# A graph-layer kernel: VectorE's queue alone in the planner's order, GpSimd's transfers ordered by the framework

## The chip, the cores and the metric

The kernel runs on one core of a Trainium2 chip. The time is device microseconds from the first to the last instruction, the median of three runs. Times inside the kernel come from one profiled execution of it.

## What is computed

There are 16 graphs of 1024 nodes with 64 channels. Layer 0 is a dense step and layer 1 a ragged one: for each node and each channel it takes three quantiles over the node's neighbours. Cut to what matters:

```
h = max(layernorm(x), 0);  x = x + (adj / max(rowsum(adj), 1)) @ h            # layer 0
h = max(layernorm(x), 0)
nb      = (adj > 0) without the diagonal                                       # layer 1
removed = every skip-th neighbour, in nodes with more than 10 (and its transpose)
agg     = 0.25 * q25 + 0.5 * q50 + 0.25 * q75   # sorted values of the neighbours left and the node itself
x = x + mask * (relu((h + agg) @ W1 + b1) @ W2 + b2)
```

Most nodes have few neighbours and a few have many: the edge probability falls with the square root of the node's number.

## The kernel before, in words

**Layer 0.** A batch is one graph. Eight row tiles of its adjacency (`at`, 128x1024, five buffers) are loaded by SyncE. ScalarE takes their signs (`sg`), VectorE turns these into lists of neighbours (`rec`, 32 MAX8 instructions a batch), TensorE transposes the tiles (`pt`), ScalarE copies them out (`att`), and TensorE multiplies by the normed features (`ps_small`). VectorE adds the residual and norms once more (`ln_v`). The rows go to two tables in DRAM: `tab` by plain transfers, and `srt`, in which the nodes of four batches are sorted by their number of neighbours, by scatters on GpSimd (`srt<-row,to`, eight a batch, 128 in all).

**Layer 1.** Four batches make a group, and there are four groups. A group reads its sorted records (`recs`), makes the indices of neighbours on VectorE (`keys`, `idx`), and is then cut into ten jobs by list length (`CAPS`). A job has T columns of 128 nodes with n-1 neighbours each. Its neighbours' rows are fetched by T(n-1) gathers on GpSimd (`places<-tab,idx`): 15, 10, 8, 14, 6, 20, 16, 18, 12 and 5 gathers in the ten jobs, with T = 1, 1, 1, 2, 1, 4, 4, 6, 6 and 5. VectorE sorts the rows with a sorting network (`rem`, then min and max between `places` and `other`) and weights them (`w`, `prod`). Then the job's `layers` follow: TensorE sums (`pt`), ScalarE copies (`ot`), TensorE (`ps_small`), ScalarE (`hid`), TensorE, ScalarE (`y`). VectorE adds the residual to `y`, and GpSimd scatters it to the output (`out_dram<-y,nodes_i`, T stores a job). The nodes with the longest lists, of all groups, are four more jobs of 88, 31, 24 and 20 gathers (`lplaces`). They use the room that layer 0 leaves, so that they start after it.

**Who sets the order.** All parts are generators, and a small planner (`Plan`) chooses at each step which of them goes on. It holds a clock for each engine, and for each tile a time at which it is expected to be ready (`at(tile)`), from costs written out by hand; `room(name, bufs)` is the time at which a buffer comes free. A generator yields the engine it needs and a time from which it wants to go on. The planner takes the one with the earliest start, then the lowest rank. Slack is given by constants that are added to `at`. Three of them stand in the change: `LOOSE` (TensorE's start of `layers`, and VectorE's addition to `y`), `ROWS` (the row scatters, the gather of a group's or a long list's adjacency rows, and the `drop` scatters) and `LATE` (the stores of `y`):

```
LOOSE = 15.0
ROWS = 7.0
LATE = 25.0
```

The order in which the planner writes the instructions is what the framework sees. On engines that are named in `manual_schedule` the queue keeps that order. On the others the framework sorts the queue by a schedule of its own. Before, VectorE (DVE) and GpSimd (Pool) are named, and TensorE, ScalarE and SyncE are the framework's.

Each engine works through its queue in order, so an instruction that waits holds all that stand behind it. Between two scatters to the same table that follow each other, the kernel writes a small memset to `turn` on GpSimd. `places` has three buffers, `S` (the job's own rows) four, `y` six.

Nearly all instructions pass through the wrapper `Timed`, so they share one line, L227, in the profile. They are told apart by their tiles.

Of the kernel before, what the change touches and what calls it, by code (L numbers as in the profile page):

```python
# [9 lines left out]
F32 = mybir.dt.float32  # L10
# [8 lines left out]
P = 128  # L19
# [190 lines left out]
INF = float("inf")  # L210
BREATH = 0.8
AHEAD = 8
SLACK = 2.0
LOOSE = 15.0
ROWS = 7.0
LATE = 25.0


class Timed:
# [13 lines left out]
class Plan:  # L233
# [24 lines left out]
    def room(self, name, bufs):  # L258

        tiles = self.slots.get(name, ())  # L260
        if len(tiles) < bufs:
            return 0.0
        old = tiles[-bufs]
        return INF if self.users[old] else max(self.used.get(old, 0.0), self.ready.get(old, 0.0))

    def at(self, *tiles):
        return max(self.ready.get(t.tensor.name, INF) for t in tiles)
# [60 lines left out]
@with_exitstack  # L328
def kernel(
    ctx: ExitStack,  # L330
    tc: tile.TileContext,
    x: bass.AP,
    adj: bass.AP,
    nodemask: bass.AP,
    w1: bass.AP,
    b1: bass.AP,
    w2: bass.AP,
    b2: bass.AP,
    out: bass.AP,
):  # L340

    nc = tc.nc
    B = x.shape[0]

    flags = ctx.enter_context(tc.tile_pool(name="flags", bufs=1))
    go = flags.tile([P, 1], I32, name="go")

    with tc.manual_schedule(engines={mybir.EngineType.DVE, mybir.EngineType.Pool}):
        list_path(tc, x, adj, nodemask, w1, b1, w2, b2, out, go)
    taken = nc.values_load(go[0:1, 0:1], min_val=0, max_val=1)
    with tc.If(taken > 0):  # L360
        with tc.For_i(0, B, 1) as b:
            dense_path(tc, b, x, adj, nodemask, w1, b1, w2, b2, out)
# [3 lines left out]
def list_path(ctx, tc, x, adj, nodemask, w1, b1, w2, b2, out, go):  # L366
# [3 lines left out]
    CO = w2.shape[1]  # L370
# [19 lines left out]
    mlp = ctx.enter_context(tc.tile_pool(name="mlp", bufs=2))  # L390
# [88 lines left out]
    new, free, room, at = plan.tile, plan.release, plan.room, plan.at  # L479
# [56 lines left out]
    def known(st, *names):  # L536

        return max(at(st[name]) if name in st else INF for name in names)
# [176 lines left out]
    def endings(pool, now):  # L715

        for b, st in enumerate(batch):
            now[0] = b
            g, gb = divmod(b, GB)
            yield "ACT", lambda: known(st, "rec", "row") if st["listed"] == NT else INF  # L720
            rec, total, row = st["rec"], st["total"], st["row"]

            for t in range(NT):
                nc.scalar.activation(
                    row[:, t, R0:R0 + 8 * NSEG], rec[:, t, :], AF.Relu, bias=before[:, t:t + 1]
                )


            yield "DVE", always
            found = new(pool, [P, NT, 8 * NSEG], BF, "found", 1)  # L730
            nc.vector.tensor_scalar(found, rec, 0.0, None, op0=OP.is_gt)
            d = new(tiny, [P, NT], F32, "d", 2)
            nc.vector.tensor_reduce(d, found, AX.X, OP.add)
            full = new(tiny, [P, NT], F32, "full", 2)
            nc.vector.tensor_reduce(
                full, found.rearrange("p t (s e) -> p t s e", e=8)[:, :, :, 7], AX.X, OP.max
            )
            nc.vector.scalar_tensor_tensor(d, full, float(STEPS[0]), d, op0=OP.mult, op1=OP.max)
            nc.vector.tensor_scalar(d, d, float(STEPS[0]), None, op0=OP.min)
            for s in STEPS[1:]:  # L740
                nc.vector.scalar_tensor_tensor(d, total, float(s), d, op0=OP.is_gt, op1=OP.add)
            free(rec)
            free(total)
            hot = new(tiny, [P, CLS, NT], BF, "hot", 2)
            nc.vector.tensor_tensor(
                hot, cls, d.unsqueeze(1).to_broadcast([P, CLS, NT]), OP.is_equal
            )
            yield "PE", lambda: max(at(hot), room("ps_small", 3))
            pc = new(ps_s, [P, HALF], F32, "ps_small", 3, users=1)
            K = CLS * NT  # L750
            flat = hot.rearrange("p c t -> p (c t)")
            nc.tensor.matmul(pc[:, :K], earlier, flat, start=True, stop=True)
            nc.tensor.matmul(pc[:, K:2 * K], ones, flat, start=True, stop=True)
            yield "DVE", lambda: at(pc) + SLACK
            base = new(tiny, [P, K], F32, "base", 2)
            nc.vector.tensor_tensor_scan(
                base, pc[:, K:2 * K], zeros[:, :K], 0.0, op0=OP.add, op1=OP.add
            )
            nc.vector.tensor_tensor(base, base, pc[:, K:2 * K], OP.subtract)
            nc.vector.tensor_tensor(base, base, pc[:, :K], OP.add)  # L760
            free(pc)
            nc.vector.tensor_tensor(base, base, flat, OP.mult)
            pos = new(tiny, [P, NT], F32, "pos", 2)
            nc.vector.tensor_reduce(pos, base.rearrange("p (c t) -> p t c", t=NT), AX.X, OP.add)
            low = new(tiny, [P, NT], I32, "low", 2)
            nc.vector.tensor_copy(low, pos)
            nc.vector.tensor_scalar(low, low, LSUB - 1, None, op0=OP.bitwise_and)
            nc.vector.tensor_scalar(
                pos, pos, float(GB), float(LSUB * gb), op0=OP.mult, op1=OP.add
            )  # L770
            to = new(pool, [P, NT], I32, "to", 2)
            nc.vector.scalar_tensor_tensor(to, low, float(1 - GB), pos, op0=OP.mult, op1=OP.add)
            for t in range(NT):
                yield "POOL", lambda: max(at(to), at(row)) + ROWS if "normed" in st else INF
                scatter(srt[g], row[:, t, :], to[:, t:t + 1], sorts[g])
            free(row)
            progress["batches"] = b + 1
# [8 lines left out]
    def scatter(dst, src, idx, others):  # L786
        if plan.last is others:
            nc.gpsimd.memset(turn, 0.0)
        ins = nc.gpsimd.indirect_dma_start(
            out=dst, out_offset=bass.IndirectOffsetOnAxis(ap=idx, axis=0),  # L790
            in_=src, in_offset=None,
        )

        for other in others:
            tc.declare_no_dep(ins.ins, other, reason="rows of their own")
        others.append(ins.ins)
        plan.last = others

    class Job:
# [160 lines left out]
        def layers(self, terms, sources):  # L960

            T, R = self.T, terms[0][0].shape[1]
            yield "PE", lambda: max(at(*sources) + LOOSE, room("y", 6), room("pt", 2))
            y = new(mlp, [P, T, CO], F32, "y", 6, users=1)
            for t0 in range(0, T, 4):
                ts = range(t0, min(t0 + 4, T))
                M = len(ts) * P
# [2 lines left out]
                pt = new(ps_t, [P, HALF], F32, "pt", 2, users=1)  # L970
# [33 lines left out]
                free(py)  # L1004
            yield "DVE", lambda: at(y) + LOOSE
            nc.vector.tensor_tensor(y, y, self.S[:, :, X1:R0], OP.add)
            if self.short:
                free(self.S)
            for t in range(T):
                yield "POOL", lambda: at(y) + LATE  # L1010
                scatter(out_rows, y[:, t, :], self.nodes_i[:, t:t + 1], scatters)
            free(y)
            progress["jobs"][self.g] += 1
# [1 line left out]
    def group(g):  # L1015
# [17 lines left out]
        )  # L1033
        nodes_i = new(grp, [P, NTAU], I32, "nodes_i", 2)
        nc.vector.tensor_copy(nodes_i, nodes)
        yield "POOL", lambda: at(nodes_i) + ROWS
        full = new(grp, [P, N], F32, "gat_rows", 1)
        gather(full, adj_rows, nodes_i[:, 0:1])
        yield "DVE", always
# [22 lines left out]
        drop = new(tiny, [P, 2, 2], F32, "drop", 2)  # L1062
# [42 lines left out]
        for e in range(2):  # L1105
# [1 line left out]
                nb, cum, skip[:, e, :], None, op0=OP.is_lt, op1=OP.add,  # L1107
                accum_out=drop[:, 0, e:e + 1],
            )
        yield "POOL", lambda: at(drop) + ROWS  # L1110
        for e in range(2):
            nc.gpsimd.indirect_dma_start(
                out=pairs[:R * TS * PW, :],
# [9 lines left out]
        for i, ts in enumerate(classes):  # L1123
            n, T = CAPS[ts[0]] + 1, len(ts)
# [8 lines left out]
    def long_lists(pool):  # L1133
# [4 lines left out]
        for l, K in enumerate(LONG):  # L1138
# [12 lines left out]
            nc.vector.tensor_tensor(nodes, node, noff[:, 1:2], OP.add)  # L1151
            nodes_i = new(pool, [P, 1], I32, "lnodes_i", 4)
            nc.vector.tensor_copy(nodes_i, nodes)
            yield "POOL", lambda: max(at(nodes_i) + ROWS, room("lat", 1))
            full = new(pool, [P, N], F32, "lat", 1)
            gather(full, adj_rows, nodes_i)
            yield "DVE", lambda: at(full)
# [61 lines left out]
    for g in range(NG):  # L1219
        plan.add(group(g), -2000)  # L1220
    with tc.tile_pool(name="lay0", bufs=2) as pool:

        for stream, first in (
            (endings, 0), (channels, 1), (products, 2), (transposes, 4), (listing, 5),
            (beginnings, 6), (loads, 7), (signs, -15),
        ):
            now = [0]
            plan.add(stream(pool, now), lambda first=first, now=now: 10 * now[0] + first)
        plan.run(lambda: progress["batches"] == B)
    with tc.tile_pool(name="long", bufs=1) as pool:  # L1230
        plan.add(long_lists(pool), -1500)
        plan.run()
# [292 lines left out]
```

## Time and profile before

| | before |
|---|---|
| time, median of 3 runs | 1949.79 us (1947.86 to 1966.94) |
| span of the profiled execution | 1953.2 us |
| busy: TensorE, VectorE, ScalarE, GpSimd | 818.3, 1252.1, 607.3, 965.2 us |
| gathers `places`, 496 | 493.1 us, mean 994 ns |
| gathers `lplaces`, 163 | 172.3 us, mean 1057 ns |
| scatters `srt`, 128 | 125.4 us, mean 980 ns |
| stores of `y`, 124 of the groups | 129.6 us, mean 1045 ns |
| `turn` memsets, 200 | median 118 ns |

The busy shares say how much of the span an engine works, not what sets the end. Layer 0 with groups 0 and 1 fills the time to about 1080 us. From there on there are the long lists and groups 2 and 3. For a change of order one must look at each stage for the waits of the engine that carries it, and at what stands behind a waiting instruction in its queue.

### The profile page before, as it was taken

The page shows a single profiled execution, that of the slowest core. Times are in us where ns is not written, and L with a number is a line of the kernel's source. Part 1 is how long each engine was busy: PE and PEld are TensorE (multiplying, and loading weights), DVE is VectorE, ACT ScalarE, POOL GpSimd, SP SyncE. Part 2 cuts the span into 40 slices and gives each one's busy share as a digit, 9 for nine tenths or more (in the row PEclk, how much of TensorE's full clock was granted, in tenths as well). Part 3 has the DMA queues.
Part 4 walks back from the last instruction along what each step waited for, and adds up shares of the span by engine and source line. Part 5 has one row for each costly group of instructions (what it writes and reads, how often), then busy time and mean ns, then how long its engine had stood idle before and what let it go on. Part 6 is the DMA issues. An engine that isn't in the chain of part 4 may idle for free.

```text
span 1953.2 us, 15147 instructions
## 1 busy us (share of the span) xinstructions
PE 818.3 (42%) x3336; PEld 518.3 (27%) x3336; DVE 1252.1 (64%) x4090; ACT 607.3 (31%) x1874; POOL 965.2 (49%) x1140
## 2 busy tenths in 40 slices
PE   6778651345688236611577001000001458142155
PEld 3334421223355013410245000000001237132134
DVE  7766877636676557954642396747935779785290
ACT  7888744225465435513333000000000011010011
POOL 0123255534434654347525625478775546747723
PEclk8978875667788678755777555555555557555556
DMA  4545633213344323422201201111111101111100
GB/s 159 160 123 167 182 103 83 64 47 75 93 123 126 91 77 117 105 74 60 56 23 37 56 19 32 30 40 22 24 27 36 25 17 25 25 43 32 24 7 14
DMA packets 119013, 129.09 MB, mean 66 GB/s; under 512 B 68306, under 2 KB 86866, under 8 KB 118914
## 3 DMA queue, kind: packets, MB, share of 16 engines
q1 hardware_dynamic: 86178, 86.58, 15.6%
q0 software_dynamic: 32736, 41.47, 9.4%
q14 instruction: 71, 0.58, 0.1%
q8 instruction: 28, 0.46, 0.1%
HBM read 108.70 MB, written 19.28 MB: 66 GB/s over the span
## 4 chain that ended last, share of the span: by engine, by line
DVE 34%; PE 16%; issue 15%; another core or an unknown queue 14%; ACT 9%; POOL 8%; DMA 2%; SPq 0%; DVEq 0%; POOLq 0%; ACTq 0%
PE ps_small L227 9%; PE pt L227 7%; DVE other L227 5%; DVE places L227 5%; DVE rec L227 4%; POOL lplaces L227 3%; POOL places L227 2%; DVE lplaces L227 2%; DVE long_other L227 2%; ACT ln_sq L227 2%; ACT sg L227 2%; DVE sg L227 2%; POOL out_dram L227 2%; ACT att L227 2%
## 5 line engine op out<-in xcount | busy, mean ns | idle before, releaser
L227 POOL DMA_INDIRECT places<-tab,idx x496 | 493.1, 994 | 263.6 <-issue 141.7
L227 PE MATMUL pt<-ident,prod 128*128 128x128 f32 (+1 forms) x736 | 155.7, 371 | 553.1 <-DVE prod L227 350.2
L227 PE MATMUL ps_small<-att,h 128*65 128x512 f32 x512 | 269.8, 677 | 63.3 <-ACT h L227 42.8
L227 PEld LDWEIGHTS pt<-ident,prod 128*128 128x128 f32 (+1 forms) x736 | 127.2, 254 | 586.0 <-issue 210.5
L227 PE MATMUL pt<-ident,at 128*128 128x128 f32 x1024 | 184.9, 329 | 170.8 <-ACT att L227 83.5
L227 POOL DMA_INDIRECT srt<-row,to x128 | 125.4, 980 | 261.0 <-ACT row L227 158.6
L227 POOL DMA_INDIRECT out_dram<-y,nodes_i x124 | 129.6, 1045 | 210.9 <-issue 72.2
L227 POOL DMA_INDIRECT lplaces<-tab,lidx x163 | 172.3, 1057 | 73.0 <-issue 47.8
L227 PEld LDWEIGHTS pt<-ident,at 128*128 128x128 f32 x1024 | 139.6, 167 | 225.0 <-ACT att L227 106.8
L227 DVE MAX8 rec<-sg 128x8 f16<-128x256 f16 x512 | 180.2, 414 | 13.2 <-remote 5.8
L227 ACT COPY att<-pt 128x512 f32<-128x512 f32 x256 | 142.3, 583 | 130.9 <-remote 79.8
L227 ACT COPY ot<-pt 128x128 f32<-128x128 f32 (+3 forms) x56 | 22.4, 399 | 426.6 <-issue 175.3
L227 ACT ACTIVATE sg<-at 128x1024 f16<-128x1024 f32 x128 | 134.9, 1055 | 40.8 <-DVE rec L227 19.0
L227 DVE TENSOR_TENSOR sg<-sg,keyed 128x1024 f16<-128x1024 f16 x128 | 87.3, 682 | 81.0 <-ACT sg L227 80.8
L227 PEld LDWEIGHTS ps_small<-att,h 128*65 128x65 f32 x512 | 78.7, 159 | 208.8 <-issue 137.8
L227 PE MATMUL ps_small<-ot,w_sb 128*128 128x128 f32 (+3 forms) x112 | 56.9, 602 | 121.7 <-ACT ot L227 89.1
L227 DVE TENSOR_TENSOR other<-places,other 128x64 f32<-128x64 f32 (+6 forms) x204 | 69.8, 342 | 39.3 <-DVE places L227 11.6
L227 PE MATMUL ps_small<-w_sb,hid 128*128 128x64 f32 x256 | 68.6, 360 | 58.4 <-issue 43.0
L227 ACT ACTIVATE y<-ps_small,recs 128x64 f32<-128x64 f32 x124 | 31.5, 312 | 187.2 <-PE ps_small L227 66.3
L227 ACT ACTIVATE wu<-wu 128x39 f32<-128x39 f32 (+9 forms) x40 | 9.4, 235 | 249.7 <-issue 130.5
L227 DVE TENSOR_TENSOR places<-places,other 128x64 f32<-128x64 f32 (+2 forms) x208 | 62.4, 309 | 25.4 <-DVE other L227 10.2
L227 PEld LDWEIGHTS ps_small<-w_sb,hid 128*128 128x128 f32 x256 | 51.1, 246 | 87.7 <-issue 53.3
(208 smaller groups left out, 1652.2 us busy)
## 6 DMA issues: line engine op xcount, KB each, us to landing
at<-in_adj_dram SPq DMA_DIRECT2D x128, 512.0 KB
places<-tab,idx POOLq DMA_INDIRECT x496
tab<-row SPq DMA_DIRECT2D x16, 264.0 KB
xt<-in_x_dram SPq DMA_DIRECT2D x16, 256.0 KB
S<-srt SPq DMA_DIRECT2D x8, 390.0 KB
lplaces<-tab,lidx POOLq DMA_INDIRECT x163
recs<-srt SPq DMA_DIRECT2D x4, 544.0 KB
S<-srt SPq DMA_DIRECT2D x8, 260.0 KB
```

What stands on the lines that cost most here:

```text
L227: ins = getattr(self._engine, op)(*args, **kwargs)
```

## The change

GpSimd is taken out of `manual_schedule`: its transfers are now ordered by the framework, as TensorE's and ScalarE's are. VectorE's queue stays in the planner's order. The three constants become one of 7.0, which brings the addition to `y` and the stores closer behind the rows they need in the plan; the gathers of adjacency rows and the `drop` scatters have no slack any more. `y` has four buffers in place of six, in the kernel and in the planner's condition. The aim is to let the framework put transfers where their data are ready, and to end a job soon after its sort, so that its buffers come free.

```
-LOOSE = 15.0
-ROWS = 7.0
-LATE = 25.0
+LOOSE = 7.0
...
-    with tc.manual_schedule(engines={mybir.EngineType.DVE, mybir.EngineType.Pool}):
+    with tc.manual_schedule(engines={mybir.EngineType.DVE}):
...
             for t in range(NT):
-                yield "POOL", lambda: max(at(to), at(row)) + ROWS if "normed" in st else INF
+                yield "POOL", lambda: max(at(to), at(row)) + LOOSE if "normed" in st else INF
                 scatter(srt[g], row[:, t, :], to[:, t:t + 1], sorts[g])
...
-            yield "PE", lambda: max(at(*sources) + LOOSE, room("y", 6), room("pt", 2))
-            y = new(mlp, [P, T, CO], F32, "y", 6, users=1)
+            yield "PE", lambda: max(at(*sources) + LOOSE, room("y", 4), room("pt", 2))
+            y = new(mlp, [P, T, CO], F32, "y", 4, users=1)
...
             for t in range(T):
-                yield "POOL", lambda: at(y) + LATE
+                yield "POOL", lambda: at(y) + LOOSE
                 scatter(out_rows, y[:, t, :], self.nodes_i[:, t:t + 1], scatters)
...
-        yield "POOL", lambda: at(nodes_i) + ROWS
+        yield "POOL", lambda: at(nodes_i)
         full = new(grp, [P, N], F32, "gat_rows", 1)
...
-        yield "POOL", lambda: at(drop) + ROWS
+        yield "POOL", lambda: at(drop)
...
-            yield "POOL", lambda: max(at(nodes_i) + ROWS, room("lat", 1))
+            yield "POOL", lambda: max(at(nodes_i), room("lat", 1))
```

## The prediction

> **What bounds the kernel now.** I read the page first (busy shares and slices), then the busy times of five stretches of the span, then VectorE's waits in two windows, then single lines of the timeline.
>
> ```profile
> PE 818.3 (42%) x3336; PEld 518.3 (27%) x3336; DVE 1252.1 (64%) x4090; ACT 607.3 (31%) x1874; POOL 965.2 (49%) x1140
> ...
> DVE  7766877636676557954642396747935779785290
> ...
> POOL 0123255534434654347525625478775546747723
> PEclk8978875667788678755777555555555557555556
> ```
> No engine is full. VectorE (DVE) is the busiest with 1252 us, but 701 us of the span it stands idle. TensorE's clock is at half for most of the second half.
>
> ```profile
> 256.00:683.00 427.00, 216.47 (x876) 129.84 (x875) 265.80 (x881) 192.78 (x604) 206.72 (x264) 0.69 0.32 88
> 683.00:1080.00 397.00, 192.73 (x779) 115.80 (x779) 223.42 (x745) 145.34 (x450) 189.87 (x237) 0.69 0.26 69
> 1080.00:1328.00 248.00, 14.21 (x50) 11.55 (x50) 154.31 (x572) 4.93 (x18) 132.16 (x150) 0.50 0.15 35
> 1328.00:1953.00 625.00, 210.45 (x906) 164.35 (x906) 417.70 (x1247) 55.58 (x175) 379.64 (x401) 0.57 0.12 25
> ```
> The columns are the stretch, its length, and busy us (instructions) of PE, PEld, DVE, ACT and POOL, then clock, DMA share and GB/s. I cut where the work changes: groups 0 and 1 beside layer 0 (256 to 1080), the keys of the long lists (1080 to 1328), the long sort with the rest of groups 2 and 3 (1328 on). In every stretch VectorE is busy for some 60%. The kernel is thus bound by waits of an in-order VectorE queue, and the question is which waits the new order adds and removes.
>
> Waits of VectorE from 960 to 1090, then from 1090 to the end (us in total, times, longest):
> ```profile
> DVE sg L227 <- ACT sg L227: 22.3, 1, 22.3
> DVE ln_v L227 <- remote: 19.4, 1, 19.4
> DVE base L227 <- PE ps_small L227: 13.1, 2, 12.6
> DVE rev L227 <- DMA srt<-row,to: 10.9, 1, 10.9
> ```
> ```profile
> DVE y L227 <- ACT y L227: 58.0, 9, 18.3
> ...
> DVE lrem L227 <- DMA lplaces<-tab,lidx: 20.2, 1, 20.2
> ...
> DVE rem L227 <- DMA places<-tab,idx: 13.9, 1, 13.9
> ```
> At the end of layer 0 the last batch's chain leaves VectorE without work. Later the largest item is the addition of the residual to `y`, which waits for ScalarE's `y`; two waits are for gathers.
>
> ```profile
> 1273.73 0.55 DVE L227 TENSOR_TENSOR prod<-other,w 128x384 f32<-128x384 f32 x1
> 1279.70 0.23 DVE L227 TENSOR_TENSOR y<-y,S 128x64 f32<-128x64 f32 x1 [5.43 <-ACT y L227]
> ...
> 1548.70 0.42 DVE L227 TENSOR_TENSOR y<-y,S 128x256 f32<-128x256 f32 x1 [6.82 <-ACT y L227]
> ```
> This is the chain that matters: from a job's last product on VectorE through TensorE, ScalarE, TensorE, ScalarE, TensorE, ScalarE to its addition. It takes 6 us for one column of 128 rows. Following job after job in the timeline of the last stretch, I find 14.5 us for two columns, 17.7 to 40.5 for four, 20 to 28 for five or six, and 19 to 39 for the long lists.
>
> [...] 0.50 from 1080 to 1328, where TensorE is busy 14 of 248 us. So the short bursts of this chain run at half clock and do not get shorter. [...] the first job's last gather ends at 254.0 in the timeline and its reader starts at 256.6. So I count 1.25 us per transfer in the queue (0.94 us and a gap of 0.30) and about 3 us until the last lands.
>
> **The change part by part.** The orders are those of the two built programs; work between two places of VectorE's queue is the sum of the median durations that the instructions standing there have in the trace of before.
>
> *GpSimd's small memsets.* All 200 move to the head of its queue. In a run of stores one costs 0.12 us with a gap of 0.19, but without it the gap is 0.30, so a store costs 1.25 us either way: nothing gained. At the head they take 24 us (200 x 0.12) to 62 us (with the gaps). The first row scatter is due at about 44 us (its index is written then) its table is read from about 193 us (group 0's `S`), and its row buffer is one of four, wanted again by the fifth batch: hidden, 0.
>
> *GpSimd's queue.* The stores now stand closer behind their jobs. For each job I compared the transfers between its last blocker and its last gather, at 1.25 us, with VectorE's work ahead of its sort. All have room in the new order; the tightest are two jobs of group 0, with some 5 us. In the old order two had none: the first long list and the 15-transfer job of group 2. Gathers should cost no wait, except by a store whose `y` is late, which the next item counts.
>
> *The `y` addition.* With LOOSE 7 for 15, VectorE's work between a job's last product and its addition falls. For the last stretch, in queue order, with transfers of the job, work before -> after, chain of before, and wait that is left (chain less work): 6: 12.8 -> 5.4, 5.9, 0.5. 20: 20.3 -> 10.2, 30.9, 20.7. 16: 20.3 -> 12.7, 17.7, 5.0. 18: 26.6 -> 17.4, 27.7, 10.3. 12: 34.1 -> 18.7, 20.1, 1.4. 10: 26.5 -> 8.2, 10.5, 2.3. 8: 16.7 -> 4.1, 5.9, 1.8. 14: 15.6 -> 4.5, 14.5, 10.0. 6: 2.9 -> 5.1, 6.6, 1.5. Long 31: 20.2 -> 18.2, 18.8, 0.6. 20: 22.8 -> 17.5, 40.5, 23.0. Long 24: 23.2 -> 22.9, 38.7, 15.8. 16: 29.3 -> 10.1, 17.7, 7.6. Long 20: 17.2 -> 10.4, 30.1, 19.7. 18: 11.9 -> 9.5, 23.9, 14.4. The sum is 135. With the shortest chain of a like shape for the 20s and the long ones (17.7 and 18.8; 22.9 hides the third) it is 72. Before had 37 at these same additions (6.8, 0.4, 3.5, 18.3, 0.9, 7.3). Net +35 to +98; I take **+66**. Behind each stands the next job's sort, and behind that its buffer and the next gathers.
>
> In groups 0 and 1 the work falls from 37 to 72 us down to 14 to 42 for most jobs, against chains of 15 to 68. Stretching work by 1.35 for the gaps there, ten additions would wait, 179 us in all; but VectorE waits for layer 0 in those stretches anyway, and layer 0's chains go on meanwhile. Between 0 and 90; I take **+25**.
>
> *Where jobs stand.* The 15-transfer job of group 2 is sorted before the last batch's index in VectorE's queue (before: after it). Its sort, 21.5 us, fills part of the 66 us of waits shown from 960 to 1090: **-21**. Group 2's 14-transfer job moves ahead of the first long list. That list's 88 gathers then have 92 transfers, 115 us, between the index and the last gather, against more than 128 us of VectorE's time there (the measured time of that part before, without this sort): the 20.2 goes. Behind it the first waiting job has 6 instead of 14 gathers, so 13.9 and two followers of 5.8 and 5.9 go: together **-46**. The moved job's addition stands right behind its product: 14.5 less 1.4, **+13**.
>
> *`y` with 4 buffers for 6; the other waits.* A fifth `y` waits for the first one's store. In the built order of the last stretch that store stands ahead of the fifth job's own gathers, so it is long done: 0. Taking ROWS from the group's gather and drop positions them earlier in the plan alone: 0 beyond the order counted.
>
> Sum: 66 + 25 - 21 - 46 + 13 = +37, so 1949.8 + 37 = **1987**.
>
> **The rivals.**
> *Faster, 1920.* Chains at their short end (+35), layer 0's slack hides all of the earlier additions (0), and the gathers give -54 net: -19; layer 0 run with sorts packed (group 0's jobs end with 80 rows listed, not 87) saves another 10. For it: most of the kernel's waits are not at `y`. Against it: the half clock.
> *No change, 1950.* The two sums cancel: +35 and +19 against -54.
> *Much slower, 2070.* The late `y` also holds stores, and gathers behind them: 98 + 90 - 67 = +121. For it: TensorE waits 350 us for VectorE's `prod` already, so what stops VectorE stops layer 0's transposes.
>
> **How the numbers follow.** The forecast has 0.40, much slower 0.15, no change 0.20, faster 0.25. From 1905 (the faster case with another 15 of layer 0) to 2070. Slower by over 1% 0.55, within 1% 0.20, faster 0.25.
>
> **What would show it.** Right: VectorE's waits for ScalarE's `y` go from 58 us to 100 to 170; the wait of `lrem` for the long gathers is under 5 us; the waits between the last listing and the long lists shrink by some 20; GpSimd's memsets all lie in the first 70 us. Wrong: `y` waits that stay near 60 (then faster), or `places` gathers whose wait for a store's `y` shows up as waits of `rem` for gathers (then slower than I say).

## The result, and the profile after

| | before | after |
|---|---|---|
| time, median of 4 runs | 1956.74 us (1947.86 to 1966.94) | 2014.78 us (2011.21 to 2028.47) |
| ratio, with 95% interval | 1 | **1.031** (1.026 to 1.036) |
| span of the profiled execution | 1953.2 us | 2009.4 us |

The change makes the kernel 3.1% slower. The page's busy times, and the busy tenths of VectorE and GpSimd:

```profile
PE 829.9 (41%) x3336; PEld 530.8 (26%) x3336; DVE 1251.1 (62%) x4090; ACT 611.5 (30%) x1874; POOL 964.4 (48%) x1140
...
DVE  7757849555447557857515395251499877947372
...
POOL 4131434736162725366346427657543547577423
```
The engines do the same work as before, and VectorE stands idle for 57 us more. New in its row are the digits 5251 in slices 25 to 28 (1206 to 1407 us); GpSimd's row has 7657 there. The stretches, cut at the same places of VectorE's queue as before (first sort, first sort of group 1, keys of the long lists, long sort):

```profile
282.00:737.00 455.00, 240.84 (x916) 142.27 (x914) 271.07 (x897) 206.69 (x641) 205.37 (x206) 0.69 0.30 84
737.00:1145.00 408.00, 191.05 (x765) 120.95 (x765) 235.27 (x792) 137.03 (x420) 200.59 (x203) 0.67 0.25 68
1145.00:1447.00 302.00, 14.92 (x56) 12.05 (x56) 144.52 (x526) 5.36 (x19) 175.06 (x182) 0.51 0.15 33
1447.00:2009.00 562.00, 203.02 (x880) 158.15 (x880) 406.45 (x1217) 54.16 (x168) 285.64 (x265) 0.58 0.10 22
```
The first sort comes at 282 us (256 before), groups 0 and 1 take 455 and 408 us (427 and 397), the last stretch 562 (625). The third, the keys of the long lists, takes 302 us for 248, though VectorE works less in it (144.5 us for 154.3) and GpSimd more (175.1 for 132.2). VectorE's waits from 1145 us to the end, then from 960 to 1145:

```profile
DVE y L225 <- ACT y L225: 90.4, 11, 26.9
DVE y L225 <- issue: 43.5, 5, 15.8
DVE lfound L225 <- remote: 20.9, 5, 9.1
DVE other L225 <- remote: 20.6, 8, 3.6
DVE other L225 <- DVE other L225: 15.8, 16, 1.2
```
```profile
DVE deg L225 <- PE ps_small L225: 45.3, 2, 33.3
DVE deg L225 <- remote: 19.7, 1, 19.7
DVE y L225 <- ACT y L225: 16.3, 1, 16.3
```
("remote" is a wait at whose end the trace shows no instruction and no transfer that had just finished. What stands behind many of these comes after e6.) No gather is waited for any more. The additions to `y` wait as forecast. What was not on the list is the last line of the first block: VectorE waits for VectorE, 16 times for a microsecond each.

**Where the 56 us are.** I add up VectorE's waits over the whole span by the tile that waits: `y`; layer 0 (`sg`, `ln_v`, `ln_s`, `deg`, `base`); gathers (`rem`, `lrem`); all others.

| us | `y` | layer 0 | gathers | others |
|---|---|---|---|---|
| before | 71 | 258 | 35 | 262 |
| after | 158 | 313 | 1 | 215 |
| difference | +87 | +55 | -34 | -47 |

The sum is +60, the span grew by 56. Most of "others" are what I call late starts: VectorE has nothing to wait for but itself, and still begins late. I count VectorE's idle time directly ahead of instructions that wait for nothing but VectorE's own semaphore, where it is over 0.25 us: 218 us before, 184 after. They have moved: in the stretch of the keys from 45 to 116 us, in the last stretch from 90 to 22. Elsewhere such instructions follow each other at once: in before's first sort `gone`, `ok`, `valid`, `q` and `wu` (256.79 to 257.67 us) each read the one before and start 0.03 to 0.04 us after its end. The timeline of VectorE in after, where the gaps are over 1 us:

```profile
1366.66 0.22 DVE L225 TENSOR_TENSOR places<-places,other 128x64 f32<-128x64 f32 x1 [1.17 <-DVE other L225]
...
1372.26 0.30 DVE L225 TENSOR_TENSOR other<-other,places 128x128 f32<-128x128 f32 x1 [1.17 <-DVE other L225]
1373.66 0.23 DVE L225 TENSOR_TENSOR other<-places,other 128x64 f32<-128x64 f32 x1 [1.10 <-DVE other L225]
1375.06 0.23 DVE L225 TENSOR_TENSOR other<-places,other 128x64 f32<-128x64 f32 x1 [1.17 <-issue]
```
Each reads what the one before wrote and starts 1.40 us after it, though the work takes 0.2 to 0.3 us. Nothing else stands between them. In windows of 20 us (the columns as in the stretches), the start of such a spell:

```profile
1185.00:1205.00 20.00, 0.00 (x0) 0.00 (x0) 18.55 (x72) 0.00 (x0) 2.00 (x3) 0.50 0.03 5
1205.00:1225.00 20.00, 0.00 (x0) 0.00 (x0) 18.92 (x58) 0.68 (x3) 15.11 (x16) 0.50 0.19 49
1225.00:1245.00 20.00, 0.00 (x0) 0.00 (x0) 7.65 (x44) 0.00 (x0) 15.12 (x17) 0.50 0.15 27
1245.00:1265.00 20.00, 0.00 (x0) 0.00 (x0) 3.60 (x15) 0.00 (x0) 15.12 (x17) 0.50 0.21 52
```
GpSimd starts the 88 gathers of the longest list at 1205 us, one every 1.25 us. For some 20 us VectorE stays at full pace, then it falls to 15 instructions in 20 us.

### The profile page after: what moved, and what is told of

It reads as the page before. It is cut to its first block, busy times and chain, and to the rows that moved or that the text cites. A ratio compares the mean times of both kernels' runs of the same rounds, so it can differ in the third digit from the quotient of the medians.

```text
span 2009.4 us, 15157 instructions
## 1 busy us (share of the span) xinstructions
PE 829.9 (41%) x3336; PEld 530.8 (26%) x3336; DVE 1251.1 (62%) x4090; ACT 611.5 (30%) x1874; POOL 964.4 (48%) x1140
## 5 line engine op out<-in xcount | busy, mean ns | idle before, releaser
L225 POOL DMA_INDIRECT places<-tab,idx x496 | 510.8, 1030 | 435.9 <-DVE prod L225 220.7
L225 PE MATMUL pt<-ident,prod 128*128 128x128 f32 (+1 forms) x736 | 161.7, 382 | 646.3 <-DVE prod L225 585.8
L225 PEld LDWEIGHTS pt<-ident,prod 128*128 128x128 f32 (+1 forms) x736 | 132.2, 263 | 682.0 <-DVE prod L225 511.4
L225 PE MATMUL ps_small<-att,h 128*65 128x512 f32 x512 | 263.0, 661 | 68.5 <-ACT h L225 35.0
L225 PE MATMUL pt<-ident,at 128*128 128x128 f32 x1024 | 190.4, 340 | 166.2 <-ACT att L225 70.1
L225 PEld LDWEIGHTS pt<-ident,at 128*128 128x128 f32 x1024 | 146.5, 174 | 215.9 <-ACT att L225 92.0
L225 POOL DMA_INDIRECT lplaces<-tab,lidx x163 | 156.4, 960 | 67.1 <-issue 49.1
L225 DVE TENSOR_TENSOR y<-y,S 128x64 f32<-128x64 f32 (+4 forms) x40 | 14.5, 363 | 158.1 <-ACT y L225 106.8
L225 DVE TENSOR_SCALAR deg<-ps_small 128x4 f32<-128x4 f32 x32 | 4.9, 152 | 119.5 <-remote 66.3
```

The lines of the kernel that those rows point to most:

```text
L225: ins = getattr(self._engine, op)(*args, **kwargs)
```

## The experiments

Two theories at first. **A**: the constants, that is the early additions to `y`, make the loss. **B**: the framework's order of GpSimd makes it. VectorE's queue depends on the planner alone: with the constants of after it is after's in both orders of GpSimd, with those of before it is before's. So the two parts can be had one at a time. e1 to e4 ran beside before on one chip, and ratios are always to before on the same chip.

**e1**, after with GpSimd back in the planner's order:
```
-    with tc.manual_schedule(engines={mybir.EngineType.DVE}):
+    with tc.manual_schedule(engines={mybir.EngineType.DVE, mybir.EngineType.Pool}):
```


> The changed kernel with GpSimd put back into the planner's order: VectorE's queue is that of the changed kernel, instruction for instruction. Theory A (the constants make the loss, through VectorE's order and its early additions to y): about 2015 us, ratio to before 1.02 to 1.04, and VectorE still waits some 150 us for y. Theory B (the framework's order of GpSimd makes it): within 1% of before, about 1955 us.

**e2**, before with GpSimd in the framework's order (the reverse edit):


> The kernel before with GpSimd alone left to the framework: VectorE's and TensorE's queues are those of before. Theory A: within 1% of before, about 1955 us, waits for y near 70 us. Theory B: about 2015 us.

**e3**, after with 15 for the slack of `layers` and of the addition to `y`; **e4**, before with 7 there:
```
-            yield "DVE", lambda: at(y) + LOOSE
+            yield "DVE", lambda: at(y) + 15.0        # e3; 7.0 in e4
```


> The changed kernel with the slack of 15 back at TensorE's layers and at the addition to y alone; stores and row scatters keep 7, y four buffers, GpSimd free. Theory A: most of the loss comes back, 1950 to 1975 us, waits for y under 90 us. Theory B: stays at about 2015 us.

> The kernel before with the slack of 7 at TensorE's layers and the addition to y alone. Theory A: 1990 to 2030 us, waits for y over 130 us. Theory B: within 1% of before.

| | ratio (95%) | keys of the long lists, us | `y` | layer 0 | gathers | others | late starts: keys, last stretch, all |
|---|---|---|---|---|---|---|---|
| before | 1 | 248 | 71 | 258 | 35 | 262 | 45, 90, 218 |
| e1 | 0.996 (0.993 to 1.000) | 240 | 132 | 273 | 60 | 143 | 13, 25, 69 |
| e2 | 1.015 (1.004 to 1.026) | 308 | 71 | 316 | 1 | 270 | 125, 76, 244 |
| after | 1.031 (1.026 to 1.036) | 302 | 158 | 313 | 1 | 215 | 116, 22, 184 |
| e3 | 1.031 (1.024 to 1.038) | 309 | 114 | 287 | 2 | 304 | all 240 |
| e4 | 1.021 (1.011 to 1.032) | 252 | 177 | 291 | 35 | 182 | all 131 |

From `y` on these are us of VectorE's waits in the profiled execution (the rows before and after are of the first pair of runs). e1 is the plainest result: with the planner's order of GpSimd the new constants cost nothing. Giving GpSimd to the framework costs 1.5% with the old constants and about 3.5% with the new ones. e3 takes 44 of the 87 us of added `y` waits back and is no faster for it. That speaks for B. But the table shows that A isn't void: in e1 the additions wait 61 us more than before (after: 87). It comes out even because the others fall by 120 us; late starts alone go from 218 to 69. And e4, another VectorE order with early additions, is 2.1% slower under the planner's order. So the costs of single parts can't be added up.

The stretch of the keys is longer by some 60 us wherever the framework orders GpSimd (e2, e3, after) and nowhere else, and that is where many of the late starts stand (125 of 244 us in e2, 116 of 184 in after). Its line in e1, then in e2:

```profile
1114.00:1354.00 240.00, 14.79 (x56) 11.96 (x56) 146.59 (x526) 5.36 (x19) 126.35 (x131) 0.51 0.16 36
```
```profile
1081.00:1389.00 308.00, 14.21 (x50) 11.55 (x50) 154.87 (x573) 4.93 (x18) 176.70 (x183) 0.50 0.15 33
```
VectorE's work is like that of after (144.5) and of before (154.3). The framework sends some 50 transfers more into it (x182 and x183 for x131): the gathers of the lists of 31 and 24 (143 `lplaces` transfers in after's stretch, 89 in e1's), which the planner puts behind, beside the long sort. (The expectations say 53 for these 55 gathers.) That is early for data which VectorE reads 337 and 407 us later. So the next question was whether gathers slow VectorE, and how.

**p1, the disputed cost by itself.** Chains of VectorE instructions, each with GpSimd work of one kind beside it (each instruction of a chain, a link, reads what the one before wrote):
```
for kind in kinds:      # "g" * 79; "gi" * 45; "i" * 70; ("g" * 12 + "i" * 6) * 5
    if kind == "g":
        nc.gpsimd.indirect_dma_start(out=A[:, n, :], ..., in_=rows, ...)
    else:
        nc.gpsimd.iota(fill, ...)
for k in range(ops):
    nc.vector.tensor_tensor(c, c, one[:, :width], OP.max)
```


> Measures the disputed cost by itself; the whole computation of the reference is left out. VectorE runs chains of instructions of 128x128, each reading what the one before wrote, beside eight kinds of GpSimd work: nearly nothing (c_alone), 79 indirect gathers of 128 rows back to back (c_burst), 45 gathers with an iota of about 1 us after each (c_spaced), 70 such iotas alone (c_iotas), 79 gathers beside instructions that do not depend on one another (c_lone), 79 gathers beside a chain of long instructions of 128x1024 (c_wide), 79 gathers beside a chain with a small memset of another tile after each link (c_breath), and packs of 12 gathers with 6 iotas between (c_packs). Theory B1 (back-to-back indirect transfers delay VectorE's own semaphores, so that only dependent instructions suffer, and only once a run of transfers has lasted some 20 us): a link of the chain takes 0.25 to 0.3 us in c_alone, c_iotas, c_spaced and c_packs, about 1.4 us in c_burst after its first 20 us, and 1.1 + 1.2 = 2.3 us in c_wide; c_lone stays at 0.2 us an instruction. Rival B2 ([...] any GpSimd work slows VectorE): c_iotas is slow too, c_lone is slow beside the transfers, and instructions last longer rather than start later. Rival B3 (the transfers cost VectorE nothing, and the stretch of the long lists' keys is longer for the order alone): every phase has 0.25 to 0.3 us a link.

The groups of the profile (busy us, mean ns, then the idle time just before them):

```profile
L104 DVE TENSOR_TENSOR c_wide<-c_wide,one 128x1024 f32<-128x1024 f32 x90 | 110.3, 1226 | 3.1
...
L104 DVE TENSOR_TENSOR c_spaced<-c_spaced,one 128x128 f32<-128x128 f32 x240 | 70.5, 294 | 8.2
L104 DVE TENSOR_TENSOR c_burst<-c_burst,one 128x128 f32<-128x128 f32 x240 | 70.4, 293 | 66.2 <-DVE c_burst L104 50.4 <-issue 7.7 <-remote 1.8
L104 DVE TENSOR_TENSOR c_packs<-c_packs,one 128x128 f32<-128x128 f32 x240 | 70.2, 293 | 8.2
L104 DVE TENSOR_TENSOR c_iotas<-c_iotas,one 128x128 f32<-128x128 f32 x240 | 70.1, 292 | 8.2
```
Only the unbroken run of gathers is slow, and the instructions don't last longer: they start later. An iota of 1 us after each gather, or 6 after each 12, is enough to keep the chain at 0.325 us a link. Links of 1.2 us don't suffer (`c_wide`); a small memset after each short link doesn't help (`c_breath` took 164 us for 200 links; link and memset alike start some 1.4 us after the instruction before). `c_breath` was late from its second link on, 5 us after its first gather. The gathers beside `c_wide` had then been over for 15 us, and no link of `c_wide` was late. `c_lone` says nothing of the lag: its second gather stood for 96.3 us, which the last section tells of. Windows of the burst (columns: length, DVE, POOL, clock, DMA share, GB/s):

```profile
42.00:62.00 20.00, 17.92 (x62) 15.43 (x16) 1.00 0.11 25
62.00:82.00 20.00, 12.98 (x45) 15.12 (x17) 1.00 0.11 25
82.00:102.00 20.00, 4.47 (x15) 15.12 (x17) 1.00 0.12 27
...
142.00:162.00 20.00, 11.51 (x40) 0.00 (x0) 1.00 0.01 2
```
It is the picture of the kernel: full pace at first, 15 links in 20 us after some 35 us, and the lag stays for 11 us after the last gather. B2 falls, since iotas are free and instructions don't last longer, and so does B3. B1 missed the wide links: it had 2.3 us for them, they take 1.26. So the lag is not added to every instruction.

**p2 and e5, on another chip.** p2 asks what sets the lag off. e5 is after with the early gathers held back:
```
+            if self.hold:                              # the lists of 31, 24 and 20
+                yield "DVE", lambda: 0.0 if progress["long"] else INF, lambda rank: -9000
+                held = new(pool, list(self.idx.shape), I32, "lheld", 4)
+                nc.vector.tensor_copy(held, self.idx)
+                self.idx = held
```


> Measures by itself what sets off the late starts; the whole computation of the reference is left out. Chains of VectorE instructions of 128x128, each reading what the one before wrote, beside: 79 gathers of 128 rows again (c_again), nothing (c_calm), 600 small ScalarE copies and no transfer (c_acts), 79 plain transfers issued by SyncE (c_loads), 60 gathers with an iota of 128x256 after each (c_gaps), 79 gathers of 64 rows (c_half), 79 gathers of which 40 are over before the chain begins (c_late), 79 gathers beside links of 128x512 (c_mid) and of 128x1 (c_tiny). Theory C1 (a run of indirect transfers itself delays the semaphores after it has lasted some 35 us): c_acts and c_loads stay at 0.325 us a link, c_late is at 1.40 us a link from its first links on, c_mid is about 1.4 us a link in its slow part. Rival C2 (the number of events counts, VectorE's with the transfers'[...]): c_late starts fast, because the 40 gathers before it met a quiet VectorE; c_acts slows too if the small copies are many enough; c_tiny goes slow sooner than c_again; c_half, with as many transfers but half the rows, slows as c_again does if each transfer counts, and later if each row does; c_gaps, at about 1.7 us a transfer, stays at 0.325 or slows late.

> After, with one edit: the indices of the long lists of 31, 24 and 20 go through a copy on VectorE that stands behind the start of the long sort, so that the framework can't send the 53 gathers of the lists of 31 and 24 into the stretch of the long lists' keys; they come beside the long sort, whose instructions are long. VectorE's queue before the long sort is that of after, instruction for instruction. Theory B1 (runs of indirect transfers beside VectorE's short dependent instructions cost the time): the slow spell of 1346 to 1410 us goes and that of 1230 to 1310 stays, so the stretch of the keys falls from 302 us to about 260, and the whole to about 1970 us, unless the later gathers cost something beside the sort. Rival B3 (the framework's order costs for other reasons, such as stores or scatters that come late): the stretch stays at about 300 us and the time within 1% of 2015 us.

Both met a chip on which before takes 1594.1 us in place of 1950 to 2030, and neither theory's numbers were to be had. There is no lag there at all. The burst of p1, repeated:

```profile
L110 DVE TENSOR_TENSOR c_again<-c_again,one 128x128 f32<-128x128 f32 x240 | 69.9, 291 | 8.2
```
All nine chains run at full pace, and in e5 the late starts are 0 us. e5 took 1694.4 us, a ratio of 1.062 (1.059 to 1.064). So on a chip without the lag a kernel with nearly all of the change is not free, and loses more than after does elsewhere. A likely reading is that before has no late starts to lose there, so that the additions to `y` (104 us of waits in e5) and the rest show in full. It is not shown: after and e1 did not run on that chip, holding the gathers back may have its own cost, and there is no profile of before from it.

The traces differ in one more thing. On that chip each gather shows 16 landings (some 126 in 10 us of the burst, a gather every 1.28 us). In p1 they thin out from 16 a gather to 1 within 50 us, and in after from 119 in 10 us at 1210 us to 9 at 1250. Where VectorE lags, the record of landings is incomplete. The reverse does not hold: beside `c_wide` it is as thin, some 10 in 10 us, and no link is late.

**q: before, after and e1 once more, on a chip of their own.** No edit; is the result one chip's?


> The kernel before, unchanged, beside after and e1 on one chip. Between chips its time went from 1594 us to 2033 us. Theory R (VectorE's late starts come where the record of events falls behind, on some chips and not on others): on a chip where each transfer shows its 16 landing events there are no late starts, before takes about 1600 us and the stretch of the long lists' keys under 230 us; on a chip that loses them it takes about 1950 us. Rival B1 (the transfers themselves delay the semaphores): the late starts are there on every chip where gathers run back to back.

> After, unchanged, on the same chip as before and e1. Theory R: on a chip with late starts, slower than before by about 3% and than e1 by about 3.5%; on one without them the 60 us of the stretch of the long lists' keys are not there, so that after and e1 are within 2% of each other in that stretch, and what is left of the difference to before comes from waits that are the same on every chip: the additions of y, the long sort's gathers. Rival B3 (the order costs in itself): after is slower than e1 by 50 us or more on either kind of chip.

> After with GpSimd back under the plan's order (e1 again), on the same chip as before and after. Theory R: as fast as before within 1% on a chip with late starts, as e1 was; on one without them slower than before by the waits of the early additions of y, some 50 us of the last two stretches, if these aren't hidden behind others. Rival: the constants cost nothing on either kind of chip.

| | ratio (95%) | keys, us | `y` | layer 0 | gathers | others | late starts: keys, last stretch, all |
|---|---|---|---|---|---|---|---|
| before | 1.000 (0.998 to 1.003) | 254 | 65 | 278 | 29 | 280 | 56, 92, 233 |
| after | 1.036 (1.030 to 1.041) | 311 | 185 | 305 | 1 | 228 | 121, 13, 204 |
| e1 | 0.996 (0.994 to 0.999) | 241 | 142 | 278 | 60 | 152 | 14, 21, 77 |

The same ratios and nearly the same split: they are the kernels', on chips that lag. On one chip, after is 3.9% slower than e1 (2041.7 for 1965.0 us). Theory R and B3 forecast alike for such a chip, so this run doesn't decide between them.

**p3 and e6.** p3 asks whether any events do it or only indirect transfers. e6 is the kernel of e5 again.


> Chains of VectorE instructions of 128x128 again, the whole computation of the reference left out: beside nothing (c_calm, c_rest, c_peace, c_quiet), 79 gathers back to back (c_again), 500 dependent ScalarE copies of 128x1 (c_acts), 1000 GpSimd memsets of 128x1 (c_pools), 600 small matmuls (c_mats), the last three together (c_every), 158 plain transfers by SyncE (c_loads), 79 gathers of 64 rows (c_half), and 79 gathers of which 40 are over before the chain begins (c_late). On a chip that records all 16 landing events of each transfer no chain is slow, as in the probe before. On one that loses them, Theory R (the record falls behind, whatever its events are): c_again slows to about 1.4 us a link after some 35 us, c_late, whose first 40 gathers met a resting VectorE, begins fast or at least faster than c_again ended, c_every or c_loads, rich in events but without an indirect transfer, slows as well. Rival B1 (indirect transfers alone do it): c_every and c_loads stay at 0.325 us a link, and c_late is slow from its first links on.

> The kernel that holds the gathers of the lists of 31 and 24 back until the long sort, again, for a chip with late starts (its first run met a chip without them). Theory B1 and Theory R alike: with 53 fewer gathers in it, the stretch of the long lists' keys falls from after's 303 to 311 us to about 260, the late starts after the second run of gathers go, and the ratio to before falls from 1.031 to 1.036 to about 1.01. If the order costs for another reason, the stretch stays above 295 us and the ratio at 1.03.

This chip lags (before 1977.0 us). From the groups of p3:

```profile
L115 DVE TENSOR_TENSOR c_every<-c_every,one 128x128 f32<-128x128 f32 x400 | 116.8, 292 | 13.6
...
L115 DVE TENSOR_TENSOR c_half<-c_half,one 128x128 f32<-128x128 f32 x240 | 70.1, 292 | 71.7 <-DVE c_half L115 54.8 <-issue 8.9 <-remote 1.8
...
L115 DVE TENSOR_TENSOR c_late<-c_late,one 128x128 f32<-128x128 f32 x160 | 46.8, 292 | 45.2 <-DVE c_late L115 34.5 <-issue 6.6
```
`c_every` had ScalarE, GpSimd memsets and TensorE beside it, and the 158 plain transfers too, which came earlier than meant. They reported some 320 landings in 10 us for most of 80 us, all in the trace, and no link was late. So R in its wide form, that any events do it, falls at these rates: of what was tried, only the transfers that GpSimd issues do it. Half the rows make no difference (71.7 us of idle time, 68.1 in `c_again`). `c_late` began 52 us into a run of gathers:

```profile
1358.10 5.17 DVE L115 TENSOR_TENSOR c_late<-c_late,one 128x128 f32<-128x128 f32 x16
1363.73 0.29 DVE L115 TENSOR_TENSOR c_late<-c_late,one 128x128 f32<-128x128 f32 x1 [0.47 <-DVE c_late L115]
1364.44 0.29 DVE L115 TENSOR_TENSOR c_late<-c_late,one 128x128 f32<-128x128 f32 x1 [0.41 <-DVE c_late L115]
1365.84 0.29 DVE L115 TENSOR_TENSOR c_late<-c_late,one 128x128 f32<-128x128 f32 x1 [1.11 <-DVE c_late L115]
```
16 links at full pace (5.17 us), then the lag: 52 us of gathers beside a quiet VectorE did not make the first links late, which B1 excluded. e6, the stretch of the keys:

```profile
1160.00:1428.00 268.00, 16.32 (x56) 12.97 (x56) 145.09 (x527) 5.36 (x19) 144.06 (x149) 0.50 0.15 33
```
It is 268 us long for 302 and 311 in after, with 149 transfers for 182 and 186 (the 55 gathers are gone, some others have come in), and the ratio is 1.014 (1.008 to 1.019) for 1.031 and 1.036. The expectation was about 260 us and 1.01. Late starts in this stretch are 64 us for 116 and 121. VectorE's queue up to here is that of after, so in the kernel itself gathers beside short dependent instructions cost time; taking 55 of them away gives back 1.7 to 2.2 points of the 3.1 to 3.6%.

**e5 and e6 side by side.** They are one program, on the chip without the lag and on one with it: 1697.8 and 2006.9 us. VectorE's late starts are 0 and 141 us, so they are less than half of the 309 us between the two. ScalarE is late as well, behind TensorE. I take its copies and activations that read TensorE's results (`att`, `ot`, `hid`, `y`, `msg`) and wait for no other engine, and look for those that begin over 1 us after both ScalarE and TensorE had ended what they had begun. e5 has none. e6 has 41, late by 272 us in all; before has 41 (267 us), after 35 (226 us), e1 38 (185 us). (Not all of it is on the path that sets the end, and the ends of matmuls in the trace are modelled.) In after it makes the longest wait at `y`:

```profile
1843.19 5.41 PE L225 MATMUL pt<-ident,prod 128*128 128x128 f32 x24 [6.33 <-DVE prod L225]
1869.00 0.59 ACT L225 COPY ot<-pt 128x512 f32<-128x512 f32 x1 [31.50 <-remote]
...
1890.34 0.42 DVE L225 TENSOR_TENSOR y<-y,S 128x256 f32<-128x256 f32 x1 [26.85 <-ACT y L225]
```
TensorE has ended at 1848.60, the copy waits for TensorE alone, and it starts 20.4 us later. Behind the addition in VectorE's queue stand steps of a long list's sort that read what VectorE had last written by 1862.84; the first of them starts at 1890.69, none in the 26.85 us before the addition. So the lag reaches the additions to `y` too: e5 waits 104 us for them and e6 189, and layer 0 waits 161 and 320.

**What stays open.** What the lag is, is not shown. Missing landings and late starts were seen together (e6's trace holds 7662 of 18768 landings, e5's 18612), but not always: beside `c_wide` landings were missing and no link was late, and the plain transfers beside `c_every`, with some 320 landings in 10 us, made no link late. All times here come from runs that record span and clock, so whether a run without any record lags, and whether the change costs 3% there, wasn't seen. Open, too, is why layer 0 waits 27 to 58 us longer under the framework's order (313 for e1's 273, 305 for 278 on one chip, 316 for before's 258).

## Why the prediction was right, and where it was wrong

Slower was forecast, 1987 us, and slower it is. The forecast sum was +37, the measured one +58. By its own terms:

- **The `y` additions**, +66, +25 and +13 for the moved job: +104 in all, measured +87. In the last stretch they wait 106 us for 53 (+54, taken +66); the moved job's addition waits 15.8 us (at 1446.98; taken +13); in groups 0 and 1 it is +24 (taken +25); at the additions of the long lists' keys it is -6. The sign that was named came: `y` waits for ScalarE 106.8 us for 58.4 (with those that the view gives to "issue", 158 for 71). But the sum fits better than its pieces. The waits at the lists of 31, 24 and 20, 36 of the forecast 135 us, did not come. That TensorE's bursts in these chains stay at half clock was an estimate from before's 0.50 and 0.57 in the last two stretches; after has 0.51 and 0.58. And the chains were taken from before as if their length were their own: of the 38.7 us for the list of 24, 27.2 lie between the end of TensorE's last transpose (1829.49) and ScalarE's copy of it (1856.67), a late start like those that e6 has and e5 has not.
- **The gathers' waits**, -46: measured -34. `lrem` and `rem` wait for none, as forecast. The two followers of 5.8 and 5.9 us were read wrongly: these are the waits ahead of `gone` (1460.5) and `other` (1474.5) in before, and both instructions wait for VectorE's own semaphore alone. They are late starts.
- **The end of layer 0**, -21: wrong. The 15-transfer job is sorted there, from 1087.6 to 1109.9 us, but the stretch is 408 us for 397 and the waits in it are new ones, `deg` for TensorE's products. The sign named for it failed: between the last listing and the long lists VectorE waits 105 us for 80. The stretch did get shorter with the planner's order (e1: 385), though that wait did not (107). In all, layer 0 waits +55.
- **GpSimd's queue**, 0: this step failed. "Gathers should cost no wait" came true for those who read them. The 3 us until a transfer lands were an estimate from one pair of times, 254.0 and 256.6: in before VectorE had begun four `rec` at 255.26 that took 1.41 us, so its next start says only that the gather had landed by then. But the step treated GpSimd's order as a matter of when data arrive. The framework's order moves some 50 transfers beside a stretch of short dependent instructions, and there, on chips that lag, VectorE itself gets slower: 54 us more for that stretch, with 71 us more of late starts.
- **What the sum had no term for** is the late starts. Before had 218 us of them, in part in plain sight as waits of VectorE for VectorE (110 us in before's view), and no step asked what they hang on. They fell by 68 in the last stretch, about what the early additions cost there, and rose by 71 in the stretch of the keys. Under the planner's order they fall in both (e1: -65 and -32).
- **The rival "much slower"** rested on TensorE, which stops for `prod`. That wait rose from 350 to 586 us, but not in layer 0 (47 before, 37 after): it did not come this way. This rival's sum also leaves out the +13 of the moved job; with it it would be +134.
- **The memsets**, 0: right, from 2.2 to 34.9 us. **`y` with 4 buffers**, 0: not tried alone; e1 has them and is not slower.

So the additions wait as forecast, and still the direction is in good part luck. In e1 they wait 61 us more than in before and the kernel is not slower; in e3 half of their added wait is gone and the kernel is as slow as after. The size is a sum of hits and misses of both signs. Of the two parts of the change it is the one priced at 0 that decides, on chips that lag: without it there is no loss (e1), and e1, at 0.996 twice, is the fastest of all versions there. Without the lag e1 was not measured.

## What to carry to other kernels

Before you let gathers run early, look at what runs beside them: on two of the three chips with a probe, chains of short instructions suffered (0.325 to 1.40 us a link); links of 1.2 us, tried on one of the two, did not. Sum an engine's waits by what they wait for, and don't skip those for the engine's own last instruction: here 16 of a microsecond each (15.8 us) were part of 184 us of late starts, and these moved when the order moved. Don't take the length of a chain from one trace for its own: look in it for gaps behind which nothing ends. And repeat on a second chip before you explain a few per cent: here the same kernel took 1594 us on one and 2033 on another.

## What was not expected of the hardware

- The lag: in p1 and p3, on two chips, a chain of short VectorE instructions falls from 0.325 to 1.40 us a link once GpSimd's indirect transfers have come every 1.25 us for 20 to 35 us, and sooner (from the second link) where a run of them had ended 15 us before; the last late starts come 10 to 18 us after the last gather. In the kernels VectorE's late starts were seen on the chip of e1 to e4 (69 to 244 us), on that of q (77 to 233) and on that of e6 (141). ScalarE, too, starts late behind TensorE, in e6 41 times and up to 29 us. On the fifth chip neither came (e5: 0 us, and none).
- In p1 VectorE wrote 480 tiles of 128x128 one after another without dependence, with no gap (97.1 us busy, 0.0 idle). GpSimd's second gather, meanwhile:

```profile
353.81 1.07 POOL L89 DMA_INDIRECT rows<-in_x_dram,idx_lone  x1 [6.25 <-DVE idx_lone L82]
355.19 96.29 POOL L89 DMA_INDIRECT rows<-in_x_dram,idx_lone  x1 [0.30 <-issue]
451.78 0.94 POOL L89 DMA_INDIRECT rows<-in_x_dram,idx_lone  x1 [0.30 <-issue]
```
It stood for 96.3 us, until VectorE was done (its last tile began at 450.4 us); beside chains with gaps of 0.03 us a gather took 0.97. What held it is not shown, nor whether a gap is what lets a gather pass.
